# First squares of whole key blocks made by VectorE out of PSUM, and token rows scattered in two chains, in a transformer layer with power attention and routed experts

## The chip, the cores and the metric

The kernel runs on one core of one Trainium2 chip. The metric is device time in microseconds (us): the median over runs of the whole kernel. A core has TensorE (PE in the profile, its weight loads PEld), VectorE (DVE), ScalarE (ACT), GpSimd (POOL) and SyncE (SP, which here only issues DMA transfers). PSUM is the memory that TensorE writes; this kernel uses it as eight banks of 128 partitions by 512 floats.

## The reference

One layer over x of 4 batches x 1,024 tokens x 128 channels, all in float32. xn is the layer norm of x; the result is x + attention(xn) + experts(xn).

```python
qkv = x @ W_attn + b_attn                      # 16 heads of 8
s = einsum('bhtd,bhsd->bhts', q, k)
s = s - s.mean(-1, keepdims=True)
mad = abs(s).mean(-1, keepdims=True) + 1e-06   # over all keys, not only the causal ones
s = where(causal, s / mad * score_gain, -1000.0)
r = maximum(s, 0.0) ** 4
y = einsum('bhts,bhsd->bhtd', r / (r.sum(-1, keepdims=True) + 1e-06), v)
attention = y @ W_proj + b_proj
# experts: the best 2 of 8 per token, weighted by a softmax over the two
x1 = x @ w1 + b1; x2 = x @ w2 + b2             # 128 -> 256
out += we * (silu((x1 * x2) @ wg + bg) @ w3 + b3)
```

The fourth power of the positive scores is what the change touches: it is made as relu, square, square.

## The kernel before

**A planner sets the order.** The kernel does not issue its work directly. Each step is a node (`add`) with a name, the engines that it may run on and an assumed duration on each, the nodes that it depends on, buffers that it takes and gives back, a rank, and an earliest time (`begin`). `Plan.run` is a list scheduler: it keeps a clock for each engine, takes again and again the node and engine with the smallest start minus a bias (`SOONER`, by name or by name and engine), ties broken by rank (plus `RANK` by name), and adds a handoff (`HOP`) and a lag of the engine (`LAG`) before a dependent may start. The instructions are then issued in that order. So each engine's queue has one fixed order, settled when the program is built, and the choice of engine for a relu or a square is the planner's as well. Where it expects TensorE to be idle it puts in matmuls on zeros (L1518, L1523; L426 is a warm-up).

**Attention** runs over 4 batches x 2 chunks of 512 queries. Heads are worked on in four groups r of four heads. Four heads fill the four groups of 32 rows of the PE array at once, so one quad of matmuls leaves four banks of scores. There are two kinds of quads:

- `up` (L997): queries on the partitions, all 1,024 keys along the free axis. Their absolute values are summed straight from the bank (abs) by DVE (L1010) or ACT (L1012); this is the mad.
- `score` (L1121): 128 keys on the partitions, queries along the free axis. These banks become the fourth power.

For scores, blocks of keys on the diagonal pass a causal mask on DVE (L1140: maximum with zero times a mask, into a tile u1), and the rest a relu on ACT (L1147) or DVE (L1149). The four heads are handled as two pairs m = 0 and 1. For each pair one square makes u from u1, both heads in one instruction of up to 1,024 elements, and a second square runs in place on u; each goes to ACT (L1172) or POOL (L1174). A score bank is given back when its relus are done. `av` bursts then add u times the values (L1197) and u1 times a one-hot column (L1188: the sum of the positive scores) into an accumulator bank; its transposition (L1065) and some small DVE and ACT steps give the normalised rows, and a projection (L1238 to L1256) ends the chunk. Chunk 1 of each batch has four whole blocks of 128 keys by 512 queries off the diagonal for each r, chunk 0 has none.

**Experts.** Tokens are routed on the chip. Each token's row (128 channels, its weight and its own number) is scattered to its two slots in the DRAM tensor xs, which was first filled with an empty pattern (fill, L743, issued by SP behind the spills of the transposed inputs). POOL issues the scatters: for each batch and each k of 2, a copy of the weights into the rows (`second`, L760), and then eight indirect DMAs (L769) of 128 rows. All 64 form one chain: each depends on the one before, its landing included. When all are done, SP loads rows (xg) and weights (w) for 36 tiles of 256 slots (`rows_in`, `load`). A tile is a transposition (xg, L1318), `up` products (L1329), ACT and DVE steps (z), a second product (L1338), silu on ACT, a third product (L1347), a scaling by the weight (ye, DVE L1359 or ACT L1362), and two accumulating indirect DMAs from POOL into DRAM (L1367). At the end the sums are read back and added.

Of the kernel before, what the change touches and what calls it, by code (L numbers as in the profile page):

```python
# [52 lines left out]
class Plan:  # L53

    HOP = 0.14
    LAG = {"PE": 0.2, "DVE": 0.085, "ACT": 0.1, "POOL": 0.045}

    SOONER = {"score": 0.42, "kappa": 0.03, "sq": -0.14, "sum": -0.18, "xg@DVE": 0.1, "wT@ACT": 0.5, "mean": -0.02, "blocks": 0.1, "wT@DVE": 0.24, "norm@ACT": -0.29, "place": 0.11, "sums": 0.53, "load": 0.55, "gate@DVE": -0.05, "relu0": 0.63, "relu2": 0.37, "score0": -0.02, "score2": 0.26, "sq2": 0.02, "ys0": -0.05, "out": 0.39, "v": 0.05, "gain": -0.08, "absq": 0.2, "abs0": 0.06, "sq0": -0.3, "proj": -0.5, "xT": 0.66, "second": -0.14, "up2": 0.03, "yT": 0.34, "bound@ACT": -0.07, "relu@ACT": 0.06, "up": 0.31, "relu0@DVE": -0.77, "mask2": 0.37, "sq@ACT": -0.61, "tbias": 0.38, "mask0": -0.08, "up0": -0.05, "abs0@DVE": -0.15, "ys2": 0.42, "headsT": 0.03, "ys@DVE": -0.55, "sq@POOL": -0.18, "weight": -0.22, "gate@ACT": -0.04, "count": -0.35, "hot": 0.78, "relu": -0.31, "k": 0.09, "turn": -0.29, "relu2@ACT": -0.1, "xT@ACT": -1.01, "fill": -0.54, "y@DVE": -0.02, "abs": -0.08, "gateT": 0.23, "abs2@DVE": 0.2, "gate": -0.02, "scatter": -0.03, "heads@ACT": 0.84, "abs@DVE": -0.18, "exp": 1.46, "av": -0.09, "rows_in": 0.81, "bound": 0.45, "xT@DVE": -1.99, "spill": -0.17, "moments": -0.02, "keys": -0.49, "heads@DVE": 0.01, "relu0@ACT": -0.94, "abs2@ACT": -0.27, "rows": 0.51, "av0": -0.55, "ys0@DVE": -0.08, "ys2@DVE": 0.22, "g": -0.08, "top": 0.12, "wT": -0.29, "xg@ACT": -0.39, "sq2@POOL": -0.6, "scale": -0.37, "relu2@DVE": -0.41, "sq2@ACT": -0.03, "reload": 1.42, "relu@DVE": -0.31, "xg": -0.06, "av2": -0.05, "ys": 0.11, "abs2": -0.02}  # L60
    RANK = {"xg": -23, "tbias": -15, "headsT": 7, "spill": -12, "blocks": 131, "std": -41, "scatter": 214, "y": -4, "exp": -23, "wT": -2, "absq": 236, "v": -4, "abs": -91, "weight": 8, "gain": 16, "keys": 101, "gates": 20, "abs2": 2, "relu0": 214, "sq2": 156, "ys0": 5, "up0": -23, "score2": 12, "av": 35, "second": 39, "score0": -3, "moments": -183, "relu2": 12, "heads": -2, "place": 21, "norm": -146, "abs0": 18, "mask0": 21, "h": 27, "sums": 16, "av0": 58, "up2": -7, "xT": -2, "gate": 14, "count": 7, "relu": -10, "stats": -3, "rows_in": -200, "q": 30, "gateT": -3, "bias": 2, "g": 125, "bound": -18, "sq": 14, "top": -58, "reload": 38, "ys2": -28, "k": -136, "up": 59, "hot": 5, "score": 33, "sum": 38, "mean": -17, "kappa": -4, "give": 32, "load": 22, "warm": -235, "ys": 1, "yT": -3, "turn": -110, "rows": -20, "av2": 21}
    MODE = {"up": "rows", "score": "rows", "av": "columns", "gate": "columns", "heads": "columns"}

    @classmethod
# [13 lines left out]
    def add(self, name, on, emit, deps=(), take=(), give=(), rank=0.0, after=0.0, begin=0.0,  # L78
            behind=()):
        n = Node(name, on, emit, deps, list(take), list(give), rank, after, begin, behind)  # L80
        self.nodes.append(n)
        return n
# [78 lines left out]
def t_dve(w):  # L161
    return 0.07 + 1.04e-3 * w
# [6 lines left out]
def t_sq(w):  # L169
    return 0.06 + 0.885e-3 * w  # L170


def t_pool(w):
    return 0.16 + 1.66e-3 * w
# [3 lines left out]
def layer_kernel(  # L178
# [63 lines left out]
    def keep(shape, name, dtype=F32):  # L242
        return const.tile(shape, dtype, name=name)
# [18 lines left out]
    def of_buf(b):  # L262
        return tiles[b.kind][b.slot]
# [239 lines left out]
    def norm(b, rank, begin, known=None):  # L503
# [90 lines left out]
            )  # L594
        return cs

    grid = [P, E, NTB]
    over = lambda t: t.unsqueeze(1).to_broadcast(grid)
    flat = lambda t: t.rearrange("p e n -> p (e n)")
# [2 lines left out]
    def route(rank):  # L602
# [131 lines left out]
        def gates(e):  # L734
# [8 lines left out]
            lambda e: nc.sync.dma_start(  # L743
                slots_d.rearrange("p (a n) c -> p a (n c)", n=FILL), empty.unsqueeze(1).to_broadcast([P, NS // FILL, FILL * WX])
            ),
            deps=list(spilled.values()), rank=rank, after=30.0,
        )

        def no_sums(e):
# [3 lines left out]
            nc.sync.dma_start(acc_d[:P, :], none[:, :C])  # L753

        zeroed = add("fill", {"SP": 2.5}, no_sums, deps=[filled], rank=rank, after=12.0)
        prev, dones = w, {}
        for b in range(B):
            for k in range(2):
                def weigh(e, k=k, b=b):
                    nc.gpsimd.tensor_copy(  # L760
                        of_buf(xn[b]).rearrange("p (i c) -> p i c", c=WX)[:, :, C], pr[:, 1 + k, b * TB : (b + 1) * TB]
                    )

                prev = add("second", {"POOL": 0.2}, weigh, deps=[prev, n1] + dones.get(b, []) + named, rank=rank)
                dones.setdefault(b, [])
                for i in range(TB):
                    def scatter(e, k=k, b=b, i=i):
                        nn = b * TB + i
                        nc.gpsimd.indirect_dma_start(  # L769
                            out=xs, out_offset=bass.IndirectOffsetOnAxis(ap=slot[:, k * NTB + nn : k * NTB + nn + 1], axis=0),  # L770
                            in_=of_buf(xn[b])[:, i * WX : (i + 1) * WX], in_offset=None,
                        )

                    prev = add(
                        "scatter", {"POOL": 1.12}, scatter, deps=[prev, w, filled], rank=rank, after=1.55,
                        give=[xn[b]] if (k, i) == (1, TB - 1) else [],
                    )
                    dones[b].append(prev)
        return [prev, tb, zeroed, n]


    q, km, Vb, sh, prepared, keyed = {}, {}, {}, {}, {}, {}
# [190 lines left out]
    def chunk(b, c, vd, sh_done, t0, t1):  # L973
# [126 lines left out]
        for r in range(NR):  # L1100
            acc = Buf("bank")
            for j, grp in enumerate(groups):
# [28 lines left out]
                scored[r].append(scores)  # L1131
                for m in range(2):
                    u1, u = u1s[m], us[m]
                    a = []
                    for g in range(2):
                        k = ks_[2 * m + g]

# [19 lines left out]
                        if rest:  # L1157
                            parts_.append(
                                add(
                                    "relu" + stage, {"ACT": t_act(rest), "DVE": t_dve(rest)}, relu, deps=[scores],  # L1160
                                    give=[] if near else [k], rank=rank - 200,
                                )
                            )
                        if near and rest:
                            add("free", {"none": 0.0}, None, deps=parts_, give=[k])
                        a += parts_
                    e1 += a
# [1 line left out]
                    def square(e, w=w, src=u1, dst=u):  # L1169
# [3 lines left out]
                        else:  # L1173
                            (nc.vector if e == "DVE" else nc.gpsimd).tensor_tensor(to, s_, s_, ALU.mult)  # L1174

                    a = add("sq" + stage, {"ACT": t_sq(2 * w), "POOL": t_pool(2 * w)}, square, deps=a, take=[u], rank=rank - 30, behind=line["sq"])
                    sq1.append(a)
                    a = add(
                        "sq" + stage, {"POOL": t_pool(2 * w), "ACT": t_sq(2 * w)},
                        lambda e, w=w, u=u, square=square: square(e, w, u, u), deps=[a], rank=rank - 30,  # L1180
                    )
                    e2.append(a)

# [372 lines left out]
```

## Time and profile before

| what | value |
|---|---|
| median of 3 runs | 901.38 us (900.55 to 901.86) |
| the profiled execution's own time | 902.11 us |
| its span, first to last instruction | 900.1 us |
| busy: PE, PEld | 880.6, 477.9 us |
| busy: ACT, POOL, DVE | 785.7, 759.9, 577.0 us |
| squares: POOL, ACT | 330, 310 instructions |
| relus: ACT, DVE | 345, 167 instructions |
| scatters (L769) | 64, from 67.8 to 270.5 us |
| first expert transposition on PE (L1318) | 278.7 us |
| granted TensorE clock, mean | 0.996 |

A span is one execution from the first to the last instruction. Busy time is the union of an engine's records; the ends of matmuls are modelled, so that a wait of part of a microsecond inside a row of matmuls does not show as idle time. In lines of groups the columns are line, engine, operation, out<-in with shapes, count, then busy us and mean ns of one, then the idle time before them and what ended it. In timeline lines they are start, duration, engine, line, operation, operands, count, and the idle time before. Lines named in the text on the kernel before are those of the listing above.

### The profile page before, as it was taken

The numbers are of one execution on the slowest core, as the hardware profiler recorded it, in microseconds if no ns is written. First come the engines' busy times: TensorE is split into PE (matmuls) and PEld (weight loads), VectorE is DVE, ScalarE is ACT, GpSimd is POOL, SyncE is SP. The second block draws the span as 40 slices with busy tenths as digits, with TensorE's granted clock in tenths as the row PEclk, the third lists the DMA queues.
The fourth block names the chain that finished last, engine by engine and source line by source line (L and its number), as shares of the span: only waits on it lengthen the run. The fifth ranks groups of instructions, "written<-read, shape, count | busy, mean of one in ns | idle before, by whom it ended". The sixth has DMA issues, their size and how long they took to land.

```text
span 900.1 us, 22539 instructions
## 1 busy us (share of the span) xinstructions
PE 880.6 (98%) x8085; PEld 477.9 (53%) x8085; DVE 577.0 (64%) x1512; ACT 785.7 (87%) x1952; POOL 759.9 (84%) x527
## 2 busy tenths in 40 slices
PE   8999999999999999999999999999999999999997
PEld 6555533334545555456466565555455666544444
DVE  7988866778767545545656655544755666565565
ACT  5789999999988889898688899989988889999985
POOL 4479898898999899999795899999868869878876
PEclk9999999999999999999999999999999999999999
DMA  4730000000005434434434354554334533532015
GB/s 111 302 103 22 22 22 23 22 23 22 23 23 157 115 94 119 104 93 112 104 76 105 78 133 100 126 133 98 89 87 108 136 75 75 139 74 69 5 12 188
DMA packets 92318, 79.20 MB, mean 88 GB/s; under 512 B 8431, under 2 KB 88366, under 8 KB 92206
## 3 DMA queue, kind: packets, MB, share of 16 engines
q1 hardware_dynamic: 79064, 68.50, 25.9%
q0 software_dynamic: 12416, 8.99, 7.1%
q8 instruction: 64, 1.05, 0.5%
q10 hardware_dynamic: 726, 0.27, 0.1%
q14 instruction: 48, 0.39, 0.1%
HBM read 58.13 MB, written 19.60 MB: 86 GB/s over the span
## 4 chain that ended last, share of the span: by engine, by line
PE 82%; POOL 7%; ACT 4%; DVE 4%; issue 2%; DMA 1%; DVEq 0%; ACTq 0%; POOLq 0%
PE bank L1121 16%; PE bank L997 16%; PE bank L1197 14%; PE bank L1188 9%; PE bank L1338 7%; PE bank L1329 7%; PE bank L1347 4%; POOL u L1174 4%; ACT bank L1012 2%; POOL xs L769 2%; PE bank L1065 2%; PE bank L1518 1%; PE bank L1318 1%; PE bank L813 1%; ACT u L1172 1%
## 5 line engine op out<-in xcount | busy, mean ns | idle before, releaser
L1174 POOL TENSOR_TENSOR u<-u 128x1024 f32<-128x1024 f32 (+1 forms) x330 | 587.1, 1947 | 61.5 <-DVE u L1140 28.9
L1172 ACT ACTIVATE u<-u 128x1024 f32<-128x1024 f32 (+1 forms) x310 | 294.2, 985 | 16.6 <-POOL u L1174 12.3
L1010 DVE TENSOR_REDUCE asum<-bank 128x1 f32<-128x512 f32 (+3 forms) x391 | 192.5, 547 | 59.0 <-PE bank L997 57.9
L1012 ACT ACTIVATE bank<-bank 128x512 f32<-128x512 f32 (+3 forms) x377 | 181.6, 482 | 20.4 <-PE bank L997 17.7
L1140 DVE SCALAR_TENSOR_TENSOR u<-bank,causal 128x256 f32<-128x256 f32 (+1 forms) x384 | 123.8, 374 | 116.4 <-PE bank L1121 90.2
L1147 ACT ACTIVATE u<-bank 128x512 f32<-128x512 f32 (+2 forms) x345 | 151.0, 501 | 43.3 <-DVE u L1140 31.0
L997 PE MATMUL bank<-blk,blk 32*128 32x512 f32 (+3 forms) x1536 | 183.9, 526 | 0.4 <-ACT bank L1012 0.4
L1121 PE MATMUL bank<-blk,blk 32*128 32x512 f32 (+3 forms) x1536 | 179.8, 528 | 0.3 <-ACT bank L1012 0.2
L1197 PE MATMUL bank<-u,V 128*32 128x512 f32 (+3 forms) x1536 | 159.5, 496 | 3.5 <-POOL u L1174 2.6
L1367 POOL DMA_INDIRECT acc<-ye,xg x72 | 113.4, 1576 | 50.6 <-ACT ye L1362 28.7
L997 PEld LDWEIGHTS bank<-blk,blk 32*128 32x128 f32 x1536 | 91.8, 184 | 83.5 <-ACT u L1147 20.2
L1149 DVE TENSOR_SCALAR u<-bank 128x512 f32<-128x512 f32 (+2 forms) x167 | 99.9, 638 | 53.8 <-PE bank L1121 52.5
L1188 PE MATMUL bank<-u,pick 128*32 128x512 f32 (+3 forms) x1280 | 124.4, 465 | 0.0
L1121 PEld LDWEIGHTS bank<-blk,blk 32*128 32x128 f32 x1536 | 64.7, 184 | 58.0 <-issue 20.5
L1188 PEld LDWEIGHTS bank<-u,pick 128*32 128x32 f32 x1280 | 42.8, 110 | 77.9 <-issue 73.5
L1197 PEld LDWEIGHTS bank<-u,V 128*32 128x32 f32 x1536 | 33.3, 108 | 91.0 <-issue 59.3
L769 POOL DMA_INDIRECT xs<-blk,slot x64 | 64.1, 1002 | 18.6 <-DMA xs<-blk,slot 8.1
L1338 PEld LDWEIGHTS bank<-z,w 128*128 128x128 f32 x576 | 67.1, 191 | 22.0 <-ACT u L1147 6.1
L1338 PE MATMUL bank<-z,w 128*128 128x128 f32 x576 | 73.7, 281 | 0.0
L1012 ACT ACTIVATION_READ_ACCUMULATOR bank<-bank 128x1 f32 x377 | 71.6, 190 | 0.0
L1329 PE MATMUL bank<-xT,w 128*128 128x128 f32 x576 | 70.3, 275 | 0.0
L1329 PEld LDWEIGHTS bank<-xT,w 128*128 128x128 f32 x576 | 67.2, 192 | 0.8 <-issue 0.8
(192 smaller groups left out, 704.2 us busy)
## 6 DMA issues: line engine op xcount, KB each, us to landing
w<-in_L_ffn_w_dram SPq DMA_DIRECT2D x216, 128.0 KB
w<-in_L_ffn_wg_dram SPq DMA_DIRECT2D x72, 256.0 KB
xs<-w SPq DMA_DIRECT2D x1, 4680.0 KB
xg<-xs SPq DMA_DIRECT2D x36, 130.0 KB
acc<-w SPq DMA_DIRECT2D x1, 2048.0 KB
blk<-acc SPq DMA_DIRECT2D x4, 512.0 KB
out_dram<-xt SPq DMA_DIRECT2D x8, 256.0 KB
xt<-in_L_attn_x_dram SPq DMA_DIRECT2D x3, 512.0 KB
```

What stands on the lines that cost most here:

```text
L997: nc.tensor.matmul(of_buf(ks_[g])[:, at : at + w], of_buf(q[b])[rows_, ii * P : (ii + 1) * P], of_buf(km[b][r])[rows_, k0 : k0 + w], start ...
L1010: nc.vector.tensor_reduce(to, of_, AX.X, ALU.add, apply_absolute_value=True)
L1012: nc.scalar.activation(of_, of_, AF.Abs, accum_out=to)
L1121: nc.tensor.matmul(of_buf(ks_[g])[:, at : at + n], of_buf(km[b][r])[rows_, jj * P : (jj + 1) * P], of_buf(q[b])[rows_, c * CH + off : (c + ...
L1140: nc.vector.scalar_tensor_tensor(of_buf(u1)[:, g, :near], of_buf(k)[:, :near], 0.0, allowed[:, :near], ALU.max, ALU.mult)
L1147: nc.scalar.activation(to, s_, AF.Relu)
L1172: nc.scalar.activation(to, s_, AF.Square)
L1174: (nc.vector if e == "DVE" else nc.gpsimd).tensor_tensor(to, s_, s_, ALU.mult)
L1188: nc.tensor.matmul(of_buf(acc)[32 * g : 32 * g + 32, off + lo : CH], pick, of_buf(u1s[g // 2])[:, g % 2, at + lo : at + n], start=begin, s ...
L1197: nc.tensor.matmul(of_buf(acc)[32 * g : 32 * g + 32, off:CH], of_buf(Vb[b])[:, jj, h0 : h0 + 32], of_buf(us[g // 2])[:, g % 2, at : at + n ...
L1329: nc.tensor.matmul(of_buf(k)[:, m * TW + j * TS : m * TW + (j + 1) * TS], weights_of(i, j)[m][:, f * P : (f + 1) * P], of_buf(tile_[i]["xT ...
L1338: nc.tensor.matmul(of_buf(k)[:, g * TW + j * TS : g * TW + (j + 1) * TS], weights_of(i, j)[2][:, f, g * P : (g + 1) * P], of_buf(tile_[i][ ...
```

## The change

Three things change.

1. For whole key blocks (no part on the diagonal) the pair m = 0 of each score quad no longer has its first square on ACT or POOL. Instead, after a head's relu has written u1, DVE reads the same score bank again and writes maximum(score, 0) times u1 into u, one instruction of 512 elements for each head (`sqv`). The second head's product comes after the first's. The bank of such a head is given back after its product instead of after its relu. The second square is as before.
2. The scatters form two chains that take turns, and the two chains are declared free of dependence on each other. The order over batches is now by pairs of batches (k = 0 of two batches, then k = 1 of the same two). Each scatter is preceded by a memset of one element, has an assumed POOL time of 1.2 instead of 1.12, a rising rank and an earliest time of 50 + 1.9 n. The assumed time of the fill falls from 30 to 18.
3. The planner's handoff falls from 0.14 to 0.06, and all values of its two tables of biases are new, so that the order on every engine is a new one.

```diff
-    HOP = 0.14
+    HOP = 0.06
-    SOONER = {"score": 0.42, "kappa": 0.03, ...
+    SOONER = {"score": 0.14, "sum": -0.28, ...
-    RANK = {"xg": -23, "tbias": -15, ...
+    RANK = {"xg": -25, "headsT": -147, ...
...
+    def apart(d, m):
+        tc.add_to_no_dep_group(f"slots{m}", d.ins)
+        tc.declare_no_dep(d.ins, group=f"slots{1 - m}", reason="no two rows go to one slot")
+    scrap = keep([1, 1], "scrap")
...
-            deps=list(spilled.values()), rank=rank, after=30.0,
+            deps=list(spilled.values()), rank=rank, after=18.0,
...
+        for b, k in [(b0 + b1, k) for b0 in range(0, B, 2) for k in range(2) for b1 in range(2)]:
...
+            weighed = add("second", {"POOL": 0.2}, weigh, deps=[w, n1] + dones[b] + named, rank=rank)
+            for i in range(TB):
+                def scatter(e, k=k, b=b, i=i, m=count % 2):
+                    nn = b * TB + i
+                    nc.gpsimd.memset(scrap, 0.0)
+                    d = nc.gpsimd.indirect_dma_start(...)
+                    apart(d, m)
+                chain = chains[count % 2]
+                chain[:] = [add(
+                    "scatter", {"POOL": 1.2}, scatter, deps=[weighed, filled] + chain, rank=rank + 0.01 * count, after=1.55,
+                    begin=50.0 + count * 1.9,
+                )]
...
+                    direct = not near and m == 0
...
-                                    give=[] if near else [k], rank=rank - 200,
+                                    give=[] if near or direct else [k], rank=rank - 200,
...
+                        if direct:
+                            def product(e, w=w, g=g, k=k, u=u, u1=u1):
+                                nc.vector.scalar_tensor_tensor(
+                                    of_buf(u)[:, g, :w], of_buf(k)[:, :w], 0.0, of_buf(u1)[:, g, :w], ALU.max, ALU.mult
+                                )
+                            squared.append(
+                                add(
+                                    "sqv", {"DVE": t_dve(w)}, product, deps=parts_ + squared, take=[] if squared else [u],
+                                    rank=rank - 200, behind=[] if squared else line["sq"],
+                                )
+                            )
+                            add("free", {"none": 0.0}, None, deps=squared[-1:], give=[k])
...
+                    if direct:
+                        a = squared
+                    else:
+                        a = [add("sq" + stage, {"ACT": t_sq(2 * w), "POOL": t_pool(2 * w)}, square, ...)]
```

## Prediction

> **What bounds the kernel now.** I read the page's busy shares and slices first, then the same by stage, then the groups of instructions, then TensorE's timeline, because a busy TensorE is not yet TensorE at its peak, and last GpSimd's timeline around the scatters.
>
> ```profile
> PE 880.6 (98%) x8085; PEld 477.9 (53%) x8085; DVE 577.0 (64%) x1512; ACT 785.7 (87%) x1952; POOL 759.9 (84%) x527
> ...
> GB/s 111 302 103 22 22 22 23 22 23 22 23 23 157 115 94 119 104 93 112 104 76 105 78 133 100 126 133 98 89 87 108 136 75 75 139 74 69 5 12 188
> ```
>
> PE is the bound by its share, with ACT and POOL close behind and DVE free for a third. The GB/s row dates the stages: 22 GB/s from 67 to 270 us is the scatters alone; the expert weights start after them.
>
> ```profile
> core 0: us, PE busy (x) PEld busy (x) DVE busy (x) ACT busy (x) POOL busy (x), PEclk, DMA share, GB/s
> ...
> 30.00:278.00 248.00, 240.29 (x2166) 115.70 (x2168) 190.52 (x472) 222.95 (x523) 218.05 (x165) 0.99 0.16 54
> 278.00:885.00 607.00, 605.03 (x5676) 336.16 (x5674) 353.38 (x916) 539.51 (x1374) 521.60 (x314) 1.00 0.41 99
> ```
>
> The first stage is attention alone, the second attention mixed with experts. ACT is at 90% in the first and 89% in the second, POOL at 88% and 86%, DVE at 77% and 58%.
>
> ```profile
> 263.06 0.71 PE L997 MATMUL bank<-blk,blk 32*128 32x256 f32 x8
> 263.70 0.70 PE L1523 MATMUL bank<-b3p,zeros 128*128 128x256 f32 x2
> ...
> 271.11 7.66 PE L997 MATMUL bank<-blk,blk 32*128 32x512 f32 x56
> 278.69 0.44 PE L1318 MATMUL bank<-ident,xg 128*128 128x128 f32 x2
> ...
> 282.72 1.14 PE L997 MATMUL bank<-blk,blk 32*128 32x512 f32 x8
> 283.79 2.05 PE L1329 MATMUL bank<-xT,w 128*128 128x128 f32 x16
> ```
>
> From start to start a quad (four heads, eight records) of 256 columns takes 0.64 (263.06 to 263.70), one of 512 columns 1.07 (282.72 to 283.79): 0.215 fixed plus 0.855 for 512 columns. The seven quads at 271.11 should take 6.2 and take 7.6: 1.4 us are lost inside a "busy" row, to score banks that are not yet drained. I did this for every burst of PE (its step to the next start, against the shortest step of that shape) and got: 4.2 before the first matmul, 838.7 of work at full speed (22.8 of it dummies, L426, L1518 and L1523), **53 of lost time**, and 4.1 of tail. Of the 53, 37.5 lie before the first expert burst (278.69) and 15.5 after it. So at most about 53 + 20 us can be won, and the question is what the change does to the 53.
>
> ```profile
> L1174 POOL TENSOR_TENSOR u<-u 128x1024 f32<-128x1024 f32 x257 | 509.9, 2142 | 58.8 <-DVE u L1140 28.0 <-ACT u L1147 13.8 <-ACT u L1172 10.0
> L1172 ACT ACTIVATE u<-u 128x1024 f32<-128x1024 f32 x255 | 262.9, 1062 | 9.8 <-POOL u L1174 7.9 <-DVE u L1149 1.1 <-DVE u L1140 0.3
> ...
> L1149 DVE TENSOR_SCALAR u<-bank 128x512 f32<-128x512 f32 x127 | 81.9, 686 | 53.8 <-PE bank L1121 52.5 <-issue 1.0
> ...
> L863 DVE TENSOR_TENSOR blk<-blk,bank 128x512 f32<-128x512 f32 x8 | 5.5, 688 | 0.4
> ```
>
> These rows price the moved work: a square is 1.06 on ACT or 1.9 to 2.1 on POOL, and a DVE operation on a full bank and an SBUF tile 0.69.
>
> **The change part by part.** Counts are those of the built changed kernel's instruction order.
>
> *Products on VectorE.* 64 first squares of 1,024 go (640 squares become 576) and 128 products of 512 come: 128 x 0.688 = 88 us of DVE. The planner then moves other work off DVE (relus 167 to 122: -28; abs 391 to 382: -5) and on to it (ye 8 to 36: +12; ys: +7.5). Sum +74, and +65 once overlap of neighbouring records is taken out as in the trace's own ratio of busy to summed time (577 of 659): DVE 642, 72%. ACT: 53 squares of 1,024 fewer (-56), relus 345 to 390 (+24), abs +6, ye -20, ys -8, copies of blk +5: -50, some -41 busy: 745, 83%. POOL: 11 large squares fewer (-21), 64 one-element memsets (the nearest row, L341's 128x1 memset, 0.10 each: +6): -16, 744, 83%. ACT and POOL together lose 57 of 1,546 us.
>
> *What it adds as a wait.* The product needs its head's relu, and the second head's product the first's; only then is the score bank freed. So a bank of those heads is held one handoff plus 0.69 longer, two banks in each of 64 quads. Behind the product on DVE's queue stand masks and abs sums, which also free banks. I take 0 on PE with experts alongside (PE ran 278 to 885 with 15.5 us lost, so other bursts stand ready) and include it in the rivals for the rest. Bounds: 0, and 64 x 0.69 = 44 us if every such quad held PE up.
>
> *Rule against the change.* The POOL squares of 1,024 take 1.90 us in the timeline whether DVE is busy or not, in the very stage where DVE runs STT (scalar_tensor_tensor) masks, one PSUM and one SBUF input:
>
> ```profile
> 100.27 1.90 POOL L1174 TENSOR_TENSOR u<-u 128x1024 f32<-128x1024 f32 x1
> 102.34 1.00 POOL L769 DMA_INDIRECT xs<-blk,slot  x1 [0.17 <-issue]
> ```
>
> The Trainium skill (GPSIMD Engine Reference, Key points) says that GpSimd shares its SBUF interfaces with VectorE and contends with VectorE instructions with two SBUF inputs or in a two-port mode. Taken as "DVE work blocks POOL", 88 us would go on POOL: 832 of some 890, 93%, the bound of the second stage. Taken literally it spares this product, whose first input is PSUM, and the trace agrees: I add 0.
>
> *Two scatter chains.* Now each of 64 scatters waits for the landing of the one before (1.60 us idle before the third here, two scatters without a square between):
>
> ```profile
> 96.66 1.00 POOL L769 DMA_INDIRECT xs<-blk,slot  x1 [0.17 <-issue]
> 99.26 0.98 POOL L769 DMA_INDIRECT xs<-blk,slot  x1 [1.60 <-DMA xs<-blk,slot]
> ```
>
> so they run about one per 3.2 us, 67.8 to 270.5, 70 squares between them. After it, pairs of scatters stand together with 23 squares between the first and last: 64 x (1.0 + 0.17 + 0.10) + 17 x 1.9 + 6 x 1.03 + 8 weight copies = 125 us. Ahead of the first scatter POOL has 39 squares and the gates (before: 16 squares), some 72 us from about 27, since the changed order starts attention of batch 0 before the other batches' norms. So the first is at about 102, the last at about 231, 40 us earlier. The fill of xs, started after the spills at about 80 and 12 us long at the 391 GB/s of the window 30 to 40 us before, is done by then. SP is passed by nothing else: the expert rows and weights still wait there for the last scatter.
>
> *But PE's order decides how much of that is used.* The first expert burst stands after 237.0 us of full-speed PE work before and after 224.4 now: 12.6 earlier, not 40. PE can't reach it before 4.2 + 224.4 = 228.6. What holds it back are ACT and POOL: up to it ACT has 283 us of summed work against 298 (z at 285.1 before; scaled: 271), POOL up to its first accumulation 256 against 278 (297.3 before; from an earlier start 271, so z about 259). The mean, 265, puts the burst some 6 us ahead of z as before: about 257. Lost time in the first stage 257 - 228.6 = 28, against 37.5. The gain is limited because the 64 scatters, POOL's 80 us, fall into a shorter stage.
>
> *The rest of PE's order.* Full-speed work 839.7 (+1.0: dummies 25.5 against 22.8, less five row bursts fewer at 0.215 and smaller items). Second stage: its long runs of key sums and scores (three quads and more) are 4, 5, 8, 7, 7 quads against 5, 7, 5, 3; at what such runs lost before (5: 1.2, 7: 1.8, 8: 2.3 to 3.9) that is 8.8 against 4.4. The other 11 I take as 7, since ACT has 511 us of busy time left for about 625 us (82%, was 89%) and POOL 83%. Sum 15 to 16. The startup (scores at about 24.8 instead of 29.9, but their relus behind four key copies on ACT) is inside the first stage's 28. Tail 4.4.
>
> Sum: 4.2 + 839.7 + 28 + 15.7 + 4.4 = 892.0 against a span of 900.1. The profiled execution's own time is 902.1, 2.0 over its span and 0.7 above the median of the three runs: 892.0 + 2.0 - 0.7 = **893.3**, against 901.4.
>
> **The rivals.**
>
> *Banks held longer (slower).* For: PE's weight loads already wait for relus to free banks (the list of waits has 20.2 us in 26 times for L997 behind ACT's relu), and DVE goes from 58% to about 71% in the second stage. Each of the 64 whole-block quads then delays PE. It decides from 8 / 64 = 0.13 us each; at 0.3 it gives 893 + 19 = 912, at 0.5 925. Against: 607 us of second stage with 15.5 lost show other bursts ready to fill in, and only 32 of the 128 products stand before the first expert burst.
>
> *Attention waits behind scatters (no change).* With two scatters ahead, a POOL square starts 2.5 us later; if memset and handoff cost 0.3 and not 0.1, POOL runs 13 us late at the last scatter and the first stage loses 37 again: 901 to 903. The same comes out if the earlier scatters are hidden anyway, behind PE's fixed order.
>
> *The lost time mostly goes (much faster).* ACT at 95% instead of 90% brings z to 258 and the burst to 251, and the second stage loses 6: 877. Against: the long runs of quads are still there.
>
> **How the numbers follow.** Forecast (884 to 899) 0.50; lost time mostly gone (below 884) 0.12; nothing gained overall (899 to 904) 0.13; banks held (above 904) 0.25. 0.2% is 1.8 us, about what this measurement can tell from no change: faster (below 899.6) 0.64, same 0.08, slower 0.28. The range 880 to 909 leaves out about a tenth on each side.
>
> **What would show it.** Right: DVE near 642, ACT near 745, POOL near 744; last scatter 225 to 240; first expert burst (xg, L1354 there) at 250 to 264; PE busy above 99% after it; products at 0.69 and POOL's squares still at 1.90. Wrong: products as releasers of PE's row bursts with several us in sum; POOL squares above 2.1 next to products; scatters spaced above 1.5 within a pair; the first expert burst after 270; a last stage with lost time above 25.

## The result, and the profile after

The changed kernel took **903.65 us** (median of 8 runs, 902.90 to 904.49), the kernel before 900.69 in the same comparison (8 runs, 899.61 to 902.72): ratio **1.0031**, 95% interval 1.002 to 1.0041. It is slower by 0.3%, where 0.9% faster had been forecast. The profiled execution has a span of 901.4 us and an own time of 903.19.

First the page of the changed kernel: busy times with their share and count, DMA traffic in the 40 slices of the span, and the shares of the chain that ended last.

```profile
PE 886.3 (98%) x8091; PEld 481.1 (53%) x8091; DVE 641.0 (71%) x1623; ACT 750.1 (83%) x1898; POOL 739.3 (82%) x579
...
GB/s 111 1 2 62 343 127 34 30 36 32 49 24 77 128 102 110 111 106 122 71 110 104 106 86 133 130 101 131 117 44 123 90 72 77 90 114 7 87 77 36
...
PE 78%; POOL 11%; ACT 4%; DVE 3%; issue 3%; DMA 1%; ACTq 0%; POOLq 0%; DVEq 0%
```

The work moved as forecast (641, 750, 739 us against 642, 745, 744), but POOL's share of the chain rose: it was 7% before. The same by stage:

```profile
30.00:278.00 248.00, 244.04 (x2124) 118.09 (x2116) 195.97 (x486) 224.74 (x549) 198.38 (x220) 1.00 0.21 69
278.00:885.00 607.00, 605.56 (x5695) 338.17 (x5687) 414.76 (x1039) 501.51 (x1295) 524.04 (x318) 1.00 0.39 97
...
30.00:265.00 235.00, 231.04 (x1988) 110.33 (x1980) 187.49 (x458) 214.71 (x520) 187.63 (x213) 1.00 0.21 71
```

The columns are PE, PEld, DVE, ACT and POOL busy, granted clock, DMA share, GB/s. The first row has the bounds of the kernel before and reaches 13 us past the changed kernel's first expert burst; the third row ends at that burst. Up to it ACT is busy for 91% (214.71 of 235 us; 90% before) and POOL for 80% (88% before). So ACT's relief lies in the second stage alone, where little time was lost anyway, and POOL's in the first brought the burst forward by less than had been forecast. The groups:

```profile
L1202 POOL TENSOR_TENSOR u<-u 128x1024 f32<-128x1024 f32 (+1 forms) x318 | 567.0, 1930 | 89.7 <-ACT u L1162 60.0 <-DVE u L1155 10.4 <-ACT u L1200 10.0
...
L1010 PEld LDWEIGHTS bank<-blk,blk 32*128 32x128 f32 x1536 | 94.3, 183 | 79.0 <-ACT bank L1025 12.0 <-DVE asum L1023 11.0 <-DVE u L1155 9.1
...
L1181 DVE SCALAR_TENSOR_TENSOR u<-bank,u 128x512 f32<-128x512 f32 x128 | 82.1, 682 | 0.6 <-POOL u L1202 0.4
```

A product takes 682 ns and waits for almost nothing. Of the 79.0 us that the weight loads of the `up` quads stand idle, the sums of absolute values end the largest parts (ACT L1025 12.0 us, DVE L1023 11.0); the products end 4.2. With the same count of bursts as in the prediction, the spans split so (us):

| | start | work at full speed | lost before the first expert burst | lost after it | tail | first expert burst |
|---|---|---|---|---|---|---|
| before | 4.2 | 838.7 | 37.4 | 15.6 | 4.1 | 278.7 |
| forecast | 4.2 | 839.7 | 28 | 15.7 | 4.4 | 257 |
| changed | 4.7 | 839.7 | **36.0** | 16.9 | 4.0 | 265.1 |

How the span splits into work and loss hangs on what counts as one shape: if the burst that follows is taken into it, the first loss is 37.2 before and 32.9 after, beside 829.4 and 833.0 of work. So the split is uncertain by some 3 us. The date of the first expert burst, 265.1 against a forecast of 257, needs no such count.

The lost time is about where it was, and its form is the same too: runs of three and more quads, nearly all of them `up`, lose 24.9 us before and 26.3 after. (A quad is counted here as eight records; one that fills its banks in two parts, of 384 and 128 columns, counts twice. Full speed for a run is 0.215 us and 0.855 for each 512 columns.) TensorE's timeline of the changed kernel shows the longest of them, and POOL's what goes on beside it (start, duration, then idle time before and its releaser):

```profile
237.13 12.87 PE L1010 MATMUL bank<-blk,blk 32*128 32x256 f32 x88
249.93 1.05 PE L1233 MATMUL bank<-u,V 128*32 128x512 f32 x4
251.42 0.62 PE L1233 MATMUL bank<-u,V 128*32 128x512 f32 x2 [0.43 <-POOL u L1202]
```

```profile
223.44 1.05 POOL L1202 TENSOR_TENSOR u<-u 128x512 f32<-128x512 f32 x1
...
230.78 0.98 POOL L776 DMA_INDIRECT xs<-blk,slot  x1 [0.48 <-issue]
...
248.48 0.96 POOL L776 DMA_INDIRECT xs<-blk,slot  x1 [0.22 <-issue]
249.46 5.59 POOL L1202 TENSOR_TENSOR u<-u 128x1024 f32<-128x1024 f32 x3
```

Eleven `up` quads, nine times 512 columns in all, take 12.87 us, of which 4.9 are lost. The last 15 scatters stand in one row from 230.8 to 249.5 with no square between them, and the `av` burst at 251.42 waits for the first square behind that row. So two things end within 2 us of each other there. ACT's timeline beside it:

```profile
242.47 0.58 ACT L1025 ACTIVATE bank<-bank 128x512 f32<-128x512 f32 x1
...
243.08 0.58 ACT L1025 ACTIVATE bank<-bank 128x512 f32<-128x512 f32 x1
...
243.68 0.58 ACT L1025 ACTIVATE bank<-bank 128x512 f32<-128x512 f32 x1
```

ACT empties one full bank per 0.60 us, and with DVE's 0.63 beside it a quad of four full banks, two for each engine, costs about 1.2 us to empty. TensorE fills them in 1.07, and in about 0.9 where quads follow each other (six times 512 columns in 5.66 us at 736.59, in the kernel with short sums of experiment 3). Some quads are narrower, but ACT's row has nothing but sums and one square until 251.06, while DVE waits there 1.3 us in sum for banks to be filled.

The scatters run from 128.4 to 248.5. They were to begin at 102: POOL's gates, which need the routing, stand at 126.6 (49.6 before), and POOL idles on the way there for relus that are not done:

```profile
69.39 0.30 POOL L550 IOTA blk<- 128x8 int32 x3
84.94 12.15 POOL L1202 TENSOR_TENSOR u<-u 128x1024 f32<-128x1024 f32 x7 [15.25 <-ACT u L1162]
102.38 14.98 POOL L1202 TENSOR_TENSOR u<-u 128x1024 f32<-128x1024 f32 x8 [5.28 <-ACT u L1162]
```

The loads of the rows for the first expert tiles are then issued in time, 14 us ahead of the first expert burst, and TensorE has no idle time just before that burst:

```profile
250.79 1.29 SPq L1326 DMA_DIRECT2D xg<-xs  x3
```

One thing more differs in the first stage, the granted clock. Two windows of the kernel before, then the same two of the changed one:

```profile
30.00:60.00 30.00, 28.32 (x250) 16.11 (x254) 28.42 (x81) 23.27 (x51) 24.04 (x17) 0.94 0.74 272
100.00:150.00 50.00, 49.83 (x410) 20.91 (x408) 37.80 (x85) 45.91 (x93) 46.37 (x35) 0.97 0.07 23
...
30.00:60.00 30.00, 28.86 (x281) 15.35 (x274) 26.00 (x70) 26.23 (x67) 21.57 (x15) 1.00 0.01 2
100.00:150.00 50.00, 49.90 (x431) 18.97 (x423) 39.98 (x92) 45.84 (x85) 44.24 (x45) 1.00 0.46 146
```

The kernel before has two stretches of 3.4 us at half clock (49.6 to 53.0 and 104.2 to 107.6), the second inside a long run of `up` quads; the changed kernel has none between its start and 899 us. They can account for up to 3.4 us of the 37.4 (an estimate: half of 6.8). The forecast gave the clock no term.

### The profile page after: what moved, and what is told of

The parts are those of the page before. It is cut to its first block, busy times and chain, and to the rows that moved or that the text cites. A ratio compares the mean times of both kernels' runs of the same rounds, so it can differ in the third digit from the quotient of the medians.

```text
span 901.4 us, 22636 instructions
## 1 busy us (share of the span) xinstructions
PE 886.3 (98%) x8091; PEld 481.1 (53%) x8091; DVE 641.0 (71%) x1623; ACT 750.1 (83%) x1898; POOL 739.3 (82%) x579
## 4 chain that ended last, share of the span: by engine, by line
PE 78%; POOL 11%; ACT 4%; DVE 3%; issue 3%; DMA 1%; ACTq 0%; POOLq 0%; DVEq 0%
PE bank L1134 15%; PE bank L1233 13%; PE bank L1010 13%; PE bank L1224 9%; PE bank L1374 8%; PE bank L1365 7%; POOL xs L776 5%; POOL u L1202 5%; PE bank L1383 4%; ACT bank L1025 1%; PE bank L1078 1%; ACT u L1162 1%; PE bank L826 1%; DMA xs<-blk,slot 1%; PE bank L1354 1%
## 5 line engine op out<-in xcount | busy, mean ns | idle before, releaser
L1202 POOL TENSOR_TENSOR u<-u 128x1024 f32<-128x1024 f32 (+1 forms) x318 | 567.0, 1930 | 89.7 <-ACT u L1162 60.0
L1200 ACT ACTIVATE u<-u 128x1024 f32<-128x1024 f32 (+1 forms) x258 | 241.1, 965 | 3.5 <-POOL u L1202 1.9
L1162 ACT ACTIVATE u<-bank 128x512 f32<-128x512 f32 (+2 forms) x390 | 170.9, 504 | 64.8 <-PE bank L1134 40.8
L1023 DVE TENSOR_REDUCE asum<-bank 128x1 f32<-128x512 f32 (+3 forms) x382 | 186.7, 545 | 53.2 <-PE bank L1010 52.1
L1025 ACT ACTIVATE bank<-bank 128x512 f32<-128x512 f32 (+3 forms) x386 | 186.7, 484 | 24.1 <-PE bank L1010 21.5
L1155 DVE SCALAR_TENSOR_TENSOR u<-bank,causal 128x256 f32<-128x256 f32 (+1 forms) x384 | 120.8, 373 | 75.2 <-PE bank L1134 45.7
L1233 PE MATMUL bank<-u,V 128*32 128x512 f32 (+3 forms) x1536 | 161.4, 496 | 1.8 <-POOL u L1202 1.5
L1010 PEld LDWEIGHTS bank<-blk,blk 32*128 32x128 f32 x1536 | 94.3, 183 | 79.0 <-ACT bank L1025 12.0
L1164 DVE TENSOR_SCALAR u<-bank 128x512 f32<-128x512 f32 (+2 forms) x122 | 76.9, 649 | 40.1 <-PE bank L1134 39.8
L1134 PEld LDWEIGHTS bank<-blk,blk 32*128 32x128 f32 x1536 | 65.2, 183 | 57.8 <-issue 15.2
L1181 DVE SCALAR_TENSOR_TENSOR u<-bank,u 128x512 f32<-128x512 f32 x128 | 82.1, 682 | 0.6 <-POOL u L1202 0.4
L1025 ACT ACTIVATION_READ_ACCUMULATOR bank<-bank 128x1 f32 x386 | 73.5, 191 | 0.0
```

What stands on the lines that cost most here:

```text
L1010: nc.tensor.matmul(of_buf(ks_[g])[:, at : at + w], of_buf(q[b])[rows_, ii * P : (ii + 1) * P], of_buf(km[b][r])[rows_, k0 : k0 + w], start ...
L1023: nc.vector.tensor_reduce(to, of_, AX.X, ALU.add, apply_absolute_value=True)
L1025: nc.scalar.activation(of_, of_, AF.Abs, accum_out=to)
L1134: nc.tensor.matmul(of_buf(ks_[g])[:, at : at + n], of_buf(km[b][r])[rows_, jj * P : (jj + 1) * P], of_buf(q[b])[rows_, c * CH + off : (c + ...
L1155: nc.vector.scalar_tensor_tensor(of_buf(u1)[:, g, :near], of_buf(k)[:, :near], 0.0, allowed[:, :near], ALU.max, ALU.mult)
L1162: nc.scalar.activation(to, s_, AF.Relu)
```

## The experiments

All ratios are to the kernel before, with 95% intervals. "Lost" is by the count of bursts.

**1. The parts under the old tables.** Are the two changes worth something by themselves, and did the late routing eat the gain of the scatters? Two of these four kernels have one part alone under the old tables, one has both parts under the old tables, and one the new tables alone.

```diff
 e_chains_only      before, with the new scatter part and the fill's 18.0
 e_products_only    before, with `direct` and its products
 e_both_old_order   the changed kernel, with
-    HOP = 0.06; SOONER, RANK: new values
+    HOP = 0.14; SOONER, RANK: old values
 e_tables_only      before, with
+    HOP = 0.06; SOONER, RANK: new values
```

> The kernel before with the two scatter chains (their order over batches, memset, 1.2, begin, fill 18) and nothing else: old planner tables and handoff. The built order has POOL's first scatter after 10 squares (16 before, 39 in the changed kernel) and the first expert burst after 790 of 4,196 matmuls (1,215 before, 1,121 in the changed kernel). Theory L (the new tables put norms and routing 77 us later, so the faster chains are eaten by their late start): scatters from about 62 to 165, first expert burst near 185, lost time of the first stage falls with its length from 37 to about 27, total about 890 (ratio 0.988). Rival R (the lost time belongs to the attention work and the 64 scatters and not to the date of the experts): first expert also near 185, but the time within 3 us of before (ratio 0.997 to 1.003).

> The kernel before with the products on VectorE and nothing else (one scatter chain, old tables and handoff). Theory L: products do no harm; ACT and POOL lose some 55 us of work, and the time is the same or some us better, ratio 0.993 to 1.000. Rival P (score banks are held longer by the product, and TensorE pays): slower, ratio 1.005 to 1.02, with TensorE's bursts L1134 and L1010 waiting on L1181 for several us in sum. Rival R: within 0.3%.

> The changed kernel with the old planner tables and handoff: products and two chains together. First expert burst after 736 of 4,207 matmuls. Theory L: first expert near 180 us and the fastest of these four, 880 to 890 us (ratio 0.977 to 0.988). Rival P: no better than the chains alone, by the price of the products. Rival R: within 0.3% of before.

> The kernel before with only the new planner tables and the handoff of 0.06: squares as before, one scatter chain. The built order has 58 POOL squares ahead of the first scatter and the first expert burst after 1,596 matmuls. Theory L: first scatter near 125, last near 330, first expert near 340 us, and 12 to 20 us slower than before (ratio 1.013 to 1.022), since experts are left with 550 us in which to fill TensorE's gaps. Rival R: within 5 us of before although the experts start 60 us later.

| | time | ratio | transposition of the first and of the last expert tile | lost before, between, behind these |
|---|---|---|---|---|
| before | 900.69 | 1 | 278.7, 840.9 | 37.4, 14.5, 1.2 |
| changed | 903.65 | 1.0031 (1.002 to 1.0041) | 265.1, 814.8 | 36.0, 15.0, 1.9 |
| chains only | 926.27 | 1.0267 (1.0239 to 1.0295) | 197.3, 815.3 | 31.1, 33.2, 9.0 |
| products only | 925.69 | 1.0263 (1.0246 to 1.028) | 274.9, 799.5 | 35.4, 18.4, 14.1 |
| both, old tables | 952.56 | 1.0572 (1.0555 to 1.059) | 198.5, 820.7 | 42.5, 36.5, 14.1 |
| new tables only | 946.62 | 1.0493 (1.0475 to 1.051) | 386.6, 904.9 | 61.6, 16.5, 4.2 |

Every mixture is 2.6 to 5.7% slower, and none is inside a range that was expected of it. (Rival P's "no better than the chains alone" fits the third, but experiment 3 shows the products to cost nothing measurable in the changed kernel.) Each runs one set of nodes under tables made for another, so these kernels don't price the parts; they price orders. But one thing they do tell: with early routing the experts begin at 197 us, near the 180 to 185 that the routing theory ("L") wanted, and the time is not 880 to 890 but 926 and 953. The last expert tile is then begun by 815 to 821, 94 and 109 us of full-speed work stand behind that (54 before, 81 in the changed kernel), and TensorE loses more than twice as much in the middle as before. The end of the first of these, in TensorE's timeline:

```profile
911.62 0.66 PE L1076 MATMUL bank<-ident,ys 128*128 128x128 f32 x4
915.40 1.09 PE L1249 MATMUL bank<-ident,yt 128*128 128x128 f32 x4 [3.12 <-DVE yt L1097]
916.28 1.92 PE L1265 MATMUL bank<-b3p,wT 128*128 128x512 f32 x2
```

**2. Early routing in the changed kernel.** One entry of each table is put back.

```diff
-    SOONER "moments": -0.99;  RANK "moments": 84
+    SOONER "moments": -0.02;  RANK "moments": -183
```

> The changed kernel with one entry of each planner table back at the value of before, that of the layer norm's moments (bias -0.99 to -0.02, rank 84 to -183), and so a new order: routing and the scatters come early again, the first expert burst stands after 821 of TensorE's matmuls instead of 1,121, and 537 matmuls instead of 401 stand after the last expert transposition (269 before the change). Routing theory (the late routing eats what the two chains bring): first expert at about 200, time 880 to 893. Filler theory (the experts are what TensorE does while attention waits, and an earlier start only uses them up sooner): first expert at about 200 too, but the attention that is left alone at the end loses 25 to 40 us, time 915 to 935.

Measured: 942.58 us, ratio 1.0469 (1.0451 to 1.0486). Scatters from 63.9 to 199.4, first expert burst at 213.1; lost 38.6 before it, 35.8 up to the transposition of the last tile (814.1), 13.1 behind. So the routing moved as wanted, and the routing theory falls a second time. The filler theory has the direction; the time lies beyond its 915 to 935, and the place is mostly another: only 13.1 are lost behind the last transposition, where it had 25 to 40, and 35.8 (15.0 in the changed kernel) while experts are still there. Since the new entries set a new order on every engine, what causes the loss in the middle stays open.

**3. One piece of work shortened, nothing moved.** These kernels have the changed kernel's order on every engine, so they tell which resource the lost time belongs to.

```diff
 f_products_short
-  of_buf(u)[:, g, :w], of_buf(k)[:, :w], 0.0, of_buf(u1)[:, g, :w]
+  of_buf(u)[:, g, :64], of_buf(k)[:, :64], 0.0, of_buf(u1)[:, g, :64]
 f_sums_short
-  of_buf(k)[:, at : at + w]
+  of_buf(k)[:, at : at + 64]
 f_pool_squares_short
+  if src is dst:
+      to, s_ = to[:, :, :64], s_[:, :, :64]
 h_both_short: the last two together
```

> The changed kernel with its own order on every engine; only the products on VectorE are made for 64 of 512 columns, about 0.13 instead of 0.68 us each (leaves out most of the first squares of those pairs). Bank theory: the product's time sits in front of the bank's release in 64 quads, so 64 x 0.55 = 35 us as an upper end and 8 to 20 as its likely size go: 884 to 896. Drain theory: only the sums that stand behind products on DVE's queue come earlier, 1 to 5 us: 899 to 903. Square theory: 0 to 3 us.

> The changed kernel with its own order on every engine; only the sums of absolute values out of the banks of the up quads read 64 columns instead of the whole part (leaves out most of the mean absolute difference). Drain theory (in the long runs of up quads TensorE waits for banks that DVE's and ACT's sums empty too slowly): the runs at 61, 237, 721, 743 and 763 us lose next to nothing, and since these hold some 15 to 26 of the 53 us lost, the time falls to 880 to 890, first expert burst at 245 to 255 (265.1). Bank theory (the products hold the score banks): at most 3 us less, first expert at 262 to 265. Square theory (av bursts wait for POOL's squares, which stand behind the scatters): at most 5 us less, as ACT gets no faster for the squares.

> The changed kernel with its own order on every engine; only GpSimd's second squares, made in place, cover 64 columns of each head, about 0.4 instead of 1.89 us (leaves out most of those squares). Square theory: POOL loses some 250 to 300 us of work, av bursts no longer wait, scatters come as early as the routing lets them: first expert 235 to 250, time 880 to 890. Drain theory: banks are emptied no faster, so the long runs of up quads still lose their 15 or more; first expert 258 to 264, time 893 to 901. Bank theory: 0 to 5 us.

> The changed kernel with its own order on every engine; the sums of absolute values read 64 columns, and GpSimd's in-place second squares cover 64 columns of each head, both at once (leaves out most of both). Two-wall theory (with either alone, the other wall stands right behind it: with short sums the run of 11 up quads ended at 239.6 us and TensorE then waited 5.9 us for a square of POOL that stood behind the last scatters): the gains of the two alone, 9.4 and 7.2 us, add up and the 5.9 us come on top with what the clock lost there, time 878 to 884, first expert burst at 247 to 252. One-wall theory (both walls are fed by the same late scatters and routing): the gains overlap, 886 to 893, first expert at 256 to 259.

| | time | ratio | first expert burst | lost before it, after it | lost in runs of 3 and more quads |
|---|---|---|---|---|---|
| changed | 903.65 | 1.0031 (1.002 to 1.0041) | 265.1 | 36.0, 16.9 | 26.3 |
| products short | 903.20 | 1.0025 (1.0017 to 1.0034) | 265.2 | 36.4, 16.7 | 26.2 |
| sums short | 894.22 | 0.9931 (0.9914 to 0.9947) | 262.6 | 33.8, 10.4 | 11.2 |
| squares short | 896.42 | 0.9957 (0.9941 to 0.9974) | 258.8 | 30.2, 15.7 | 26.2 |
| sums and squares short | 879.36 | 0.9758 (0.9742 to 0.9774) | 248.5 | 19.8, 8.7 | 11.2 |

The products cost nothing measurable: the bank theory falls, with the rival of the prediction that rested on it. The sums alone take 15 us of loss out of the long runs, but only 9 arrive, less than the drain theory wanted (880 to 890) and more than its rivals allowed. With squares short the time and the first expert burst are inside the ranges of the drain theory (893 to 901, 258 to 264), not of the square theory. TensorE's timeline and the windows with short sums show where the rest went:

```profile
230.59 9.11 PE L1010 MATMUL bank<-blk,blk 32*128 32x256 f32 x88
239.63 1.05 PE L1233 MATMUL bank<-u,V 128*32 128x512 f32 x4
246.56 1.07 PE L1233 MATMUL bank<-u,V 128*32 128x512 f32 x2 [5.89 <-POOL u L1202]
```

```profile
240.00:247.00 7.00, 1.11 (x8) 0.20 (x8) 0.00 (x0) 0.38 (x1) 6.32 (x9) 0.82 0.14 48
247.00:252.00 5.00, 5.00 (x28) 1.62 (x20) 0.00 (x0) 1.06 (x1) 5.00 (x4) 0.56 0.29 80
```

The eleven quads take 9.11 instead of 12.87, and then the burst of `av` waits 5.89 us for the square behind the scatters. In the changed kernel the long run covers that wait up to 0.43 us. And it costs twice: in the 5 us after it the granted clock is 0.56. With squares short alone the run of quads is 12.87 as ever. With both:

```profile
225.72 9.12 PE L1010 MATMUL bank<-blk,blk 32*128 32x256 f32 x88
234.77 1.07 PE L1235 MATMUL bank<-u,V 128*32 128x512 f32 x8
...
PE 94%; ACT 3%; DVE 1%; issue 0%; DMA 0%; ACTq 0%
```

No wait is left there, the chain (last line, from the page) is TensorE at 94%, and the 24 us gained are more than the 9.4 and 7.2 together. The two-wall theory holds, within its 878 to 884 and with the first expert burst within its 247 to 252. How much of the second wall is the scatters and how much the squares themselves was not tried: it would take short sums together with fewer scatters.

**4. Fewer scatters.**

```diff
                     nc.gpsimd.memset(scrap, 0.0)
+                    if k:
+                        return
```

> The changed kernel with its own order on every engine; the 32 scatters of k = 1 are left out, their memsets stay (leaves out half of the expert rows). Scatter theory (POOL's squares and the expert rows wait behind the back-to-back scatters of 230 to 249 us): 32 x 1.17 = 37 us of POOL's time go, some 19 of them in that last row, so no av burst waits there; but TensorE's 11 up quads at 237 still drain at 12.9 us: first expert burst at 257 to 261, time 895 to 899. Late-rows theory (the expert burst is held by the rows from DRAM): first expert at 245 to 252, 887 to 893. If neither holds, 902 to 904.

Measured: 902.87 us, ratio 1.0017 (1.0007 to 1.0026): about 1 us, as expected for the case that neither theory holds (902 to 904; 2.3 us less are lost before the first expert burst, and the tail is 1.9 longer). POOL is free 21 us earlier, at 228.48:

```profile
226.33 2.14 POOL L775 MEMSET scrap<- 1x1 f32 x15
228.48 8.44 POOL L1204 TENSOR_TENSOR u<-u 128x1024 f32<-128x1024 f32 x5
```

and TensorE's eleven quads take 12.87 us from 236.55 as before, with the first expert burst at 263.1. So while the drain of the banks stands, 37 us of scatters hardly matter.

**5. The same work in other queues' order.** TensorE's order is kept; the orders on ACT, DVE and POOL, and the engine of a relu, sum or square here and there, are set anew in both kernels.

```diff
         self.pads(order)
-        return order
+        for i, e in self.ON.items():
+            self.nodes[i].engine = e
+        return [self.nodes[i] for i in self.LINE]
```

> The changed kernel with the same work and TensorE's order untouched; only the orders on ACT, DVE and POOL, and the engine of a relu, sum or square here and there, are rearranged, by a search over the planner's own durations with a handoff of 0.10 to 0.16 us instead of 0.06. Order theory (the 53 us that TensorE loses are owed to how the other queues stand to its order): lost time falls by 6 to 12, time 891 to 898. Volume theory (the other engines have too much to do in the first stage whatever their order): lost time stays, 901 to 906.

> The kernel before, rearranged in the same manner: same work, TensorE's order untouched, the orders on ACT, DVE and POOL set by the same search. Order theory: it gains as much as the changed kernel does, 891 to 897, and the two kernels stay within 4 us of each other, so that the change itself is worth about nothing beside the order. Rival (the change gives slack that only its tight handoff hides): this one gains less than 3 us, 898 to 901, and the rearranged changed kernel is clearly ahead of it.

Measured: changed 918.02, ratio 1.018 (1.0163 to 1.0197); before 903.82, 1.003 (1.0018 to 1.0042). Both expectations missed for both kernels. The rearranged changed kernel loses 45.7 and 24.0 us instead of 36.0 and 16.9, 30.3 of them in the long runs; it has 421 sums on DVE instead of 382. An order set by assumed durations and handoffs did not find what drains the banks better. Why the changed kernel lost 14 us by it and the other 3 is not settled. A part may be the clock: up to its first expert burst the rearranged changed kernel has 13.7 us at half clock (from 23.2, 60.7 and 132.4) where the changed one has none, so up to 6.8 us (an estimate), while the kernel before goes from 6.8 us at half clock to 10.2.

**6. The walls in the kernel before.** Were the two walls made by the change? The edits are those of 3.

> The kernel before with its own order on every engine; the sums of absolute values read 64 columns (leaves out most of the mean absolute difference). Common-wall theory (the drain of the up banks cost the kernel before as much: its runs of three and more up quads lose 24.9 us, those of the changed kernel 26.3): it gains 8 to 12 us, time 889 to 893. Hidden-gain theory (the heavier load on VectorE made the drain the wall of the changed kernel alone): it gains at most 4, 897 to 901.

> The kernel before with its own order on every engine; GpSimd's in-place second squares cover 64 columns of each head (leaves out most of them). Common-wall theory: it gains 5 to 9 us as the changed kernel did, 892 to 896. Hidden-gain theory (with the single chain of scatters the squares fill gaps in which POOL waits for a landing anyway, so they cost nothing here): at most 3 us, 898 to 901.

> The kernel before with its own order on every engine; both pieces shortened at once (leaves out most of both). Common-wall theory: it gains the 24 us of the changed kernel, 875 to 880, so that the change is worth nothing with the walls away either. Hidden-gain theory: without the walls the single chain of scatters, which can go no faster than 2.6 us each, still holds the first expert burst at 255 or later: 883 to 889, and the changed kernel (879.4) is 4 to 10 us ahead.

| | time | ratio | first expert burst | lost before it, after it |
|---|---|---|---|---|
| sums short | 894.12 | 0.9924 (0.9906 to 0.9943) | 279.5 | 37.7, 7.7 |
| squares short | 894.61 | 0.9933 (0.9917 to 0.995) | 270.8 | 29.5, 14.7 |
| both | 881.41 | 0.9792 (0.9776 to 0.9809) | 265.6 | 23.6, 7.0 |

The kernel before gains 6.6, 6.1 and 19.3 us where the changed one gained 9.4, 7.2 and 24.3. Of the common-wall theory's ranges only that for the squares was met (892 to 896); 894.12 lies 1 us above its range for the sums, and 881.41 between the two theories' ranges for both. So the walls are common in the main. What is left is a small hidden gain: with both walls shortened the changed kernel is ahead, 0.9758 / 0.9792 = 0.9965 or 3 us (1 to 5 by the two intervals), where it is 3 us behind with the walls in place. Which of the three changes makes it was not tried. The clock is a rival: with both short the kernel before still has 6.8 us at half clock in its first stage and the changed one none, worth up to 3.4 us (an estimate, half of 6.8). Against it, the kernel before with short squares took 893.57 and 895.31 us in executions with a mean clock of 0.999, and 894.57 and 894.66 with 0.995 and 0.996.

## Why the prediction was wrong

**Right:** the engines' loads to 5 us; the product at 0.68; POOL's squares of 1,024 beside the products (median 1.91 us for the 70 that overlap a product, 1.90 for the other 176). That is the literal reading of the Trainium skill's GPSIMD Engine Reference, Key points, whose wider reading would have had POOL at 832: it is 739. Right too: nothing for the banks held longer. Weight loads of `up` and `score` quads do wait 9.9 us in sum for products (4.2 and 5.7), which was named as a sign of being wrong, but with the products short the time is only 0.45 us less. TensorE's full-speed work (839.7), the loss after the first expert burst (15.7, measured 16.9) and the length of the scatters (125, measured 120) came as forecast.

**Wrong, with little weight:** the scatters' start, 102 against 128.4. I laid POOL's 39 squares end to end from 27 us. POOL waited for relus instead (15.25 us in one place), and the routing came at 126.6, since the new order makes the norms of the other batches late; with the entry of the moments put back (2) the scatters begin at 63.9. But early routing did not make the kernel faster (2), half of the scatters were worth about 1 us (4), and the loads of the expert rows were issued 14 us before their first use.

**Wrong, and decisive:** the term "lost time in the first stage 257 - 228.6 = 28". It measured 36.0; the 8 us are all of the forecast gain and most of the 9.4 by which the span missed (901.4 for 892.0). I took the date of the first expert burst from ACT's and POOL's summed work, in proportion, and averaged the two, as if the loss shrank with their load. POOL's half of the average failed: POOL is busy for 80% instead of 88% up to the burst, and the burst did not come earlier for it. ACT's proportion alone gave z at 271, and z came at 269.9. That is no proof that ACT's load sets the date, and may be luck: short squares on POOL move the burst to 258.8 with ACT's work as it was.

Where the 36.0 us lie: 18.3 in runs of three and more quads (20.5 before), and short sums halve that to 9.0. So half of it is the drain of the `up` banks by the sums, which the change does not touch. Close behind stand POOL's second squares with scatters before them. Sums and squares together make up 16.2 of the 36.0 (19.8 are left in that stage with both short). For those 19.8 no cause is shown.

Three workings of the prediction slip. The mean of 265, 6.4 us behind the burst as before, puts the burst at 258.6 and not at 257, so its own working gives a loss of 30 and a span of 894. The end of the scatters is 102 + 125 = 227 and not 231. And the run of seven quads at 271.11 loses 2.2 us and not 1.4, as it holds six times 512 columns (5.34 us at full speed). I used the loss of such runs for the second stage, but not for the first. The runs there are of 5, 3, 3, 9, 3, 3, 4, 11 and 4 quads in the changed order and of 5, 3, 4, 5, 7, 8, 6, 7 and 8 in the old one: 45 against 53. At the old order's mean loss (20.5 / 53 = 0.39 us) that is a fall of about 3 us, an estimate; 2.2 were measured in this half of the loss, and 9 had been forecast for the whole.

The rival "attention waits behind scatters" gave the time nearest to the measured one (901 to 903) and named one of the two walls. That is luck in part: the dearer memset and handoff that it rested on did not come (scatters in a row stand 1.26 to 1.30 us apart, 1.27 had been forecast), and with half of the scatters gone the time stayed.

The spans of the two profiled executions are 1.3 us apart (901.4 and 900.1: 0.5 of start, 1.0 of dummies and other work, less 0.2 elsewhere), the medians 3. The rest lies in which executions were profiled: that of the kernel before was 1.4 us above its median, that of the changed one 0.5 below. Which part of the change makes the 3 us is not shown.

## To carry to other kernels

Split the lost time of the engine that bounds by the kind of burst in which it is lost, and ask of each kind whether the change touches what it waits for; a lower load elsewhere is no gain by itself. When two waits end within a microsecond or two of each other, removing either shows only a part (9.4 and 7.2 us here, of 24.3): shorten each piece of work alone and then both, without moving an instruction, before pricing a change against either. And where a planner's tables were made for one set of nodes, as here, parts of a change run under other tables price the order and not the part.

## What the hardware showed beside

- A wait of TensorE of 5.89 us cost more than itself: the granted clock was 0.56 in the 5 us behind it, and two records of `av` took 1.07 us instead of 0.62. At the end of the kernel with the chains alone a wait of 3.12 us was followed by a projection burst of 1.92 us (L1265 there), where the same burst at 892.26 us took 1.13. The clock was already down before that wait was over: it is 0.73 in 913.0 to 915.4 and 0.50 behind. The Trainium skill (TensorE: Matmul & The Clock Gate, Part 1) has the array fall to half its clock after an idle window of about 3.4 us. The wait of 5.89 us agrees with that. The second shows that a shorter wait can be enough, and the kernel before has a stretch at half clock (104.2 to 107.6) behind 3.4 us in which TensorE's records leave no gap. What decides there stays open.
- ACT's sums of 64 columns stand about 0.2 us apart where they follow each other, those of 512 columns 0.60 (the row of the accumulator's read-out, 0.18 to 0.19 us, follows each): a short sum costs a third of a full one and not an eighth.
